# A two-layer kernel: gen's product between qk's halves, av's first half a step later, spread weights a step sooner, turns by transposes, k and v without padding

## The chip, the core and the metric

One core of a Trainium2 chip runs the whole program. Its engines work side by side, each through its own instructions in order: PE (matrix products; PEld is its weight load), DVE (elementwise work and reductions), ACT (scalar functions and copies), POOL (here it issues the gathers) and SP (here it issues DMAs). They wait for each other by semaphores. The metric is device time in microseconds (us) of one execution; the median of the runs is compared. The profile is of one more execution, and its records give each instruction's start and duration.

## What is computed

The input x has 8 images of 256 channels and 64 x 64 positions, in float32. Two layers, each x + f(norm(x)), norm being a group norm over 32 groups:

```python
# layer 0, per image: attention over 3 x 3 windows plus a generated 3 x 3 convolution, 4 heads
qkv = einsum('oc,bchw->bohw', w_qkv, norm(x));  q, k, v = split(qkv)
logits = einsum('bhdl,bhdkl->bhkl', q, patches(k));  attn = softmax(logits, axis=2)
kernel = einsum('hkc,bhcl->bhkl', w_kg, qkv grouped by head) + b_kg
out = alpha * einsum(kernel, patches(v)) + beta * einsum(attn, patches(v))
x = x + einsum('oc,bchw->bohw', w_proj, out)
# layer 1, per image: a deformable 3 x 3 convolution
om = conv3x3(norm(x), w_off) + b_off            # 18 offsets and 9 masks per position
v  = bilinear sample of norm(x) at 9 shifted places (4 corners each), times sigmoid(mask)
x  = x + einsum('bckhw,ock->bohw', v, w)
```

## The kernel before

**Tiling.** An image lies in SBUF as two tiles of 128 channels (`ct`, `m`) by 4096 positions. Both layers go through it in 8 chunks `c` of 8 rows (512 positions, 4 blocks of 128, or 8 squares of 8 x 8 in attention).

**Layer 1** works in *slots*: 72 per image, one for each chunk and each of the 9 places of the window. Per slot, POOL issues four gathers (`gather`, L820: 128 positions with four corners of 256 channels each), ACT scales the first corner (`scale`, L836), DVE adds the other three (`sum_corners`, L844, three instructions for each of two blocks, six in a group), PE turns the four blocks (`transposes`, L865, eight transposes called pt), ACT copies them to vt (L868), and PE multiplies by the weights (`product`, L890, po). At the end of a chunk po is copied to y (L901), added to the residual (L906) and stored.

**Layer 0** (class `Attention`) has per chunk: `q` (L304), `k` and `v` (`keyed`, L336, each in two steps of four rows, 66 columns wide with the padding), `products` (L375) in two halves, sixteen small products each, whose results two DVE products (L383) mask into qk, `logits` (L394 to L403, DVE), `generated` (gen, L409, and its copy gs, L417), softmax in three parts, `turned` (gt, L427, four products with a constant that also adds the two channel tiles up, and DVE's addition of the bias, L435, to kb), `weights` (L495), `spread_weights` (wk, four products L508 and four DVE products L516), `keys` (transposes of v, L531, copied by ACT, L536), `weighted` (av, L549, in two halves) and `project` (L561, added by DVE, L572).

**Order.** The program's order on PE, ACT, DVE and POOL is written out by hand. `attention` and `prepare` (which puts the normed image into the gather table, computes offsets, L702, turns them, L718, and finds `positions`, L735 and on) are generators; each `yield` ends a step, 144 steps an image. The loop at the end puts one step of the *next* image into each half-slot, behind that half's `ahead` (two scales, six sums, two gathers) and `product`. In the loop's first image a step more is taken now and then, until the steps are 12 ahead (`STEPS_AHEAD`). A chunk's attention has 14 steps and so 7 slots; some parts of chunk c-1 (`d`) are done in the steps of chunk c. Before the loop, the first image's 144 steps run alone (the prologue).

The steps of a chunk before are: spread weights of d; q; k(0); k(1); products(0); products(1) with d's first av; logits with d's keys(1); generated, softmax_1; v(0); d's second av, turned; v(1), softmax_3; project(0); weights, project(1); keys(0).

**PSUM.** All of layer 0's products take their banks in turn from a pool of four (`psum_a`): a product waits until the fourth bank before it has been read. pt has two banks, po two.

Of the kernel before, what the change touches and what calls it, by code (L numbers as in the profile page):

```python
# [17 lines left out]
P = 128  # L18
# [5 lines left out]
R = 8  # L24
# [28 lines left out]
STEPS = 2 * SLOTS  # L53
STEPS_AHEAD = 12


@with_exitstack
def preact_kernel(ctx: ExitStack, tc: tile.TileContext, a: dict, out: bass.AP):
# [52 lines left out]
    gmat = const_tile("gmat", [P, P])  # L111
    bkg = const_tile("bkg", [P, HEADS * KK])
    w_qkvT = const_tile("w_qkvT", [P, NT, 3 * C])
# [9 lines left out]
    b_off = const_tile("b_off", [P, 1], nc.sync)  # L123
    stk_om = const_tile("stk_om", [P, NOM], nc.sync)
    stk_gen = const_tile("stk_gen", [P, HEADS * KK], nc.sync)
    base = const_tile("base", [P, NC * NB, 2 * KK], nc.sync)
# [15 lines left out]
    kt = const.tile([P, NT, R + 2, WP], F32, tag="k", name="k")  # L142
    vt = const.tile([P, NT, TC, KT, KT], F32, tag="v", name="v")

    w_effT = const.tile([P, NT, P // 2], F32, tag="w_effT", name="w_effT")
# [116 lines left out]

    def tiled(ps, rows):

        t = ps[:, : rows * WP].rearrange("p (r w) -> p r w", w=WP)
        t = t[:, :, 0 : TC * T].rearrange("p r (t x) -> p t r x", x=T)
        ap = [list(d) for d in t.ap]
        ap[-1][1] = KT
        return bass.AP(tensor=t.tensor, offset=t.offset, ap=ap)

# [19 lines left out]
    class Attention:  # L290
# [37 lines left out]

        def keyed(self, which, i, to):

            for lo, hi in [(0, 2)] * (self.c == 0 and i == 0) + [(2 + 4 * i, 6 + 4 * i)]:
                for m in range(NT):
                    ps = psum_a(f"ps{'qkv'[which]}_{self.u}_{lo}_{m}")
                    o = which * C + m * P
                    for ct in range(NT):
                        nc.tensor.matmul(  # L336
                            ps[:, : (hi - lo) * WP],
                            w_qkvT[:, ct, o : o + P],
                            self.xn[:, ct, lo:hi, :],
                            start=(ct == 0),  # L340
                            stop=(ct == NT - 1),
                        )
                    to(m, lo, hi, ps)

        def k(self, i):
            self.keyed(
                1,
                i,
                lambda m, lo, hi, ps: nc.scalar.copy(
                    kt[:, m, lo:hi, :].rearrange("p r w -> p (r w)"), ps[:, : (hi - lo) * WP]  # L350
                ),
            )

        def v(self, i):
            self.keyed(
                2,
                i,
                lambda m, lo, hi, ps: nc.scalar.copy(vt[:, m, :, lo:hi, :], tiled(ps, hi - lo)),
            )

# [44 lines left out]
        def generated(self):  # L405

            ps = psum_a(f"gen_{self.u}")
            for ct in range(NT):
                nc.tensor.matmul(  # L409
                    ps[64 * ct : 64 * ct + 64, :],  # L410
                    w_effT[:, ct],
                    window(self.xn, ct, 4),
                    start=True,
                    stop=True,
                )
            self.gs = gs = p1.tile([P, N], F32, tag="gs", name=f"gs_{self.u}")
            nc.scalar.copy(  # L417
                gs.rearrange("p (t y x) -> p y t x", y=T, x=T),
                ps.rearrange("p (y t x) -> p y t x", y=T, x=T),
            )  # L420

        def turned(self):

            ps = psum_a(f"gt_{self.u}")
            n = HEADS * KK
            for j in range(NB):
                nc.tensor.matmul(  # L427
                    ps[:, j * n : (j + 1) * n],
                    self.gs[:, j * P : (j + 1) * P],
                    stk_gen,  # L430
                    start=True,
                    stop=True,
                )
            self.kb = kb = p1.tile([P, self.G, KK], F32, tag="kb", name=f"kb_{self.u}")
            nc.vector.tensor_add(  # L435
                kb.rearrange("p (j h) k -> p j (h k)", j=NB),
                ps[:, : NB * n].rearrange("p (j k) -> p j k", j=NB),
                bkg.unsqueeze(1).to_broadcast([P, NB, n]),
            )
# [146 lines left out]
    def attention(b):  # L586
# [12 lines left out]
        for c in range(NC):  # L599
            a_ = Attention(b, c, xn, stats)  # L600
            if d:
                d.spread_weights()
            yield None
            a_.q(0)
# [6 lines left out]
            a_.products(0)  # L611
            yield None
            a_.products(1)
            if d:
                d.weighted(0)
            yield None
            a_.logits()
            if d:
                d.keys(1)
                d.carry_v()  # L620
            yield None
            a_.generated()
            a_.softmax_1()
# [21 lines left out]
            yield None  # L645
            a_.keys(0)
            yield None
            d = a_
        d.spread_weights()
        yield None  # L650
# [19 lines left out]
    def prepare(b, gn):  # L670
# [43 lines left out]
        def positions(c, om):  # L714
            u = f"{b}_{c}"
            ps = psum_a(f"omt_{u}")
            for j in range(NB):
                nc.tensor.matmul(  # L718
                    ps[:, j * NOM : (j + 1) * NOM],
                    om[:, j * P : (j + 1) * P],  # L720
                    stk_om,
                    start=True,
                    stop=True,
                )
            omt = ps[:, : NB * NOM].rearrange("p (b o) -> p b o", o=NOM)
            S = [P, NB, 2 * KK]

            def small(name, shape=S, dt=F32):
                return p1.tile(shape, dt, tag=name, name=f"{name}_{u}")

            mk = small("mk", [P, NB, KK])
            nc.scalar.activation(mk, omt[:, :, 18:27], AF.Sigmoid)
# [138 lines left out]
    def product(b, n, m):  # L871

        c, k = divmod(n, KK)
        if k == KK // 2 and m == 0:
            r = p1.tile([P, NT, N], F32, tag="r", name=f"r_{b}_{c}")
            if b + 1 < B:
                nc.sync.dma_start(r, kept[b % 2][:, :, c * N : (c + 1) * N])
            state["r"] = r
        if k == 0 and m == 0:

            if b + 1 == B and c % 2:
                state["po"] = [psum_a(f"po_{b}_{c}_{i}") for i in range(NT)]
            else:
                po = ps_o.tile([P, NT, 512], F32, tag="o", name=f"po_{b}_{c}")
                state["po"] = [po[:, i, :] for i in range(NT)]
        po, v = state["po"], state["v", n]
        if m == NT - 1:
            del state["v", n]
        for ct in range(NT):
            nc.tensor.matmul(  # L890
                po[m],
                w_conv[:, ct, k, m * P : (m + 1) * P],
                v[:, ct, :],
                start=(k == 0 and ct == 0),
                stop=(k == KK - 1 and ct == NT - 1),
            )

    def finished(b, c, m):
# [4 lines left out]
    def stored(b, c, m=slice(0, NT)):  # L903
        r, y = state["r"][:, m], state["y"][:, m]
        x1 = r if b + 1 < B else image[:, m, c * N : (c + 1) * N]
        nc.vector.tensor_add(r, y, x1)  # L906
        nc.sync.dma_start(
            out[b].rearrange("(t p) l -> p t l", p=P)[:, m, c * N : (c + 1) * N], r
        )
# [7 lines left out]
    with tc.manual_schedule(engines=ordered):  # L917
# [4 lines left out]
        steps = fronts()  # L922
        done = 0
        while done < STEPS:
            next(steps, None)
            done += 1
        for i in range(GATHERS):
            gather(i)
        for i in range(0, SUM_AHEAD, 2):
# [6 lines left out]
            gather(i + GATHERS)  # L936
            gather(i + GATHERS + 1)
        gather(SUM_AHEAD + GATHERS)
        gather(SUM_AHEAD + GATHERS + 1)
        last = None  # L940
        for n in range(B * SLOTS + 1):
# [3 lines left out]
            for m in range(NT):  # L945
# [16 lines left out]
                h = NT * n + m + 1  # L962
                goal = h * STEPS + min(h, STEPS) * STEPS_AHEAD
                while (done - STEPS) * STEPS < goal:
                    next(steps, None)
# [3 lines left out]
def _constants():  # L969
# [16 lines left out]
    turn_x = turns[p % T % 3]  # L986
    stk_om = np.zeros((P, NOM), f)
    for g in range(4):
        stk_om[32 * g : 32 * g + NOM] = np.eye(NOM, dtype=f)
    base = np.zeros((P, NC * NB, KK, 2), f)  # L990
# [8 lines left out]
        "turn_x": turn_x,  # L999
        "stk_om": stk_om,  # L1000
        "stk_gen": np.tile(np.eye(P // 2, HEADS * KK, dtype=f), (2, 1)),
        "base": base.reshape(P, NC * NB, 2 * KK),
# [4 lines left out]
def _laid_out(x, w_qkv, w_kg, b_kg, alpha, beta, w_proj, w_off, b_off, w):  # L1007
# [3 lines left out]
    boff = np.zeros((P, 1), np.float32)  # L1011
    boff[:NOM, 0] = b_off
    return {
        "x": x.reshape(x.shape[0], C, L),
        "w_qkvT": w_qkv.reshape(3 * C, NT, P).transpose(2, 1, 0),
        "w_qkv": w_qkv.reshape(8, 96, C).transpose(1, 0, 2),
        "w_kgT": w_kg.reshape(HEADS, KK, 2, 96).transpose(3, 0, 2, 1).reshape(96, 8, KK),
        "bkg": np.broadcast_to(b_kg.reshape(1, HEADS * KK), (P, HEADS * KK)),
        "alpha": np.broadcast_to(alpha.reshape(1, 1), (P, 1)),
# [26 lines left out]
```

## Time and profile before

| | |
|---|---|
| three timed runs | 5461.75, 5472.33, 5480.27 us; median 5472.33 |
| the profiled execution | 5417.27 us, its span 5415.5 us |
| granted PE clock, mean | 0.942 |
| first product of layer 1 | at 332.6 us |
| image 0 in layer 1 (image 1 in layer 0) | 665.0 us |
| images 1 to 6 in layer 1 | 3900 us, 650 each |
| image 7 in layer 1, nothing beside it | 517.4 us |

Busy time by stage, us (the mean clock and DMA share behind):

| stretch | PE | DVE | ACT | POOL | clock | DMA |
|---|---|---|---|---|---|---|
| 0 to 310 | 273.2 | 178.9 | 101.3 | 2.5 | 0.98 | 0.28 |
| 332.6 to 997.6 | 615.7 | 529.4 | 313.9 | 376.5 | 0.95 | 0.76 |
| 997.6 to 4897.6 | 3576.7 | 3108.8 | 1818.3 | 2218.9 | 0.95 | 0.77 |
| 4897.6 to 5415 | 379.3 | 351.0 | 207.2 | 362.2 | 0.85 | 0.76 |

How to read what follows. A line of groups names the source line, engine, operation, the tiles written and read, shapes and count, then busy time, mean duration of one and idle time before it. Durations of PE overlap, so its cost is better read from one start to the next. A float32 product stands in the trace as two records, a transpose as one. The idle time before an instruction stands in brackets with what ended it; "issue" is time in which the engine waited for nothing that the profile shows, "remote" a signal that the profile cannot put down to an engine.

### The profile page before, as it was taken

What the parts mean: (1) busy time and instruction counts of PE and PEld (TensorE: products, weight loads), DVE (VectorE), ACT (ScalarE), POOL (GpSimd) and SP (SyncE); (2) the same over time, 40 slices, a digit from 0 to 9 for tenths busy, and PEclk for the clock granted to TensorE, in tenths of its full rate; (3) what the DMA queues carried; (4) which work ended last, traced back from release to release, by engine and by line L of the source; (5) the groups of instructions that cost most, each with busy time, mean ns of one, the idle gap of its engine ahead of it and who ended that gap; (6) DMA issues with size and microseconds to landing.
All of it is one profiled execution on the core that took longest, in us unless ns stands there. A gap on an engine that the chain in (4) does not pass through costs nothing. (4 is left out here: it accounts for less than half of the span.)

```text
span 5415.5 us, 80013 instructions
## 1 busy us (share of the span) xinstructions
PE 4849.9 (90%) x26848; PEld 2762.1 (51%) x26848; DVE 4185.3 (77%) x10066; ACT 2447.4 (45%) x5312; POOL 2976.4 (55%) x2310
## 2 busy tenths in 40 slices
PE   8989999999898999999999998989999899987777
PEld 5545554555545555555555555455554555543333
DVE  5577878787787877878788787877878787777666
ACT  3344444444444444444444444444444444444343
POOL 0045554655555556455555555565654655656776
PEclk9999999999999999999999999999999999998888
DMA  2177779777697778877788777877779777688877
GB/s 91 55 253 259 253 244 330 245 249 271 242 330 270 254 264 286 307 249 262 251 310 286 265 256 256 313 266 263 260 244 332 249 248 265 235 288 307 306 268 264
DMA packets 472650, 1414.24 MB, mean 261 GB/s; under 512 B 46815, under 2 KB 114655, under 8 KB 472109
## 3 DMA queue, kind: packets, MB, share of 16 engines
q0 software_dynamic: 331776, 1208.11, 63.4%
q1 hardware_dynamic: 138444, 197.65, 10.3%
q8 instruction: 211, 3.46, 0.2%
q10 hardware_dynamic: 2016, 3.38, 0.2%
q14 instruction: 203, 1.65, 0.1%
HBM read 1276.02 MB, written 132.94 MB: 260 GB/s over the span
## 5 line engine op out<-in xcount | busy, mean ns | idle before, releaser
L820 POOL DMA_INDIRECT g<-table,idx x2304 | 2973.9, 1291 | 2418.0 <-DVE s L844 808.9
L844 DVE SCALAR_TENSOR_TENSOR s<-g,wt,s 128x256 f32<-128x256 f32 x6912 | 2811.7, 476 | 307.6 <-ACT s L836 240.7
L890 PE MATMUL po<-vt,w_conv 128*128 128x512 f32 x4608 | 2255.0, 616 | 33.9 <-ACT y L901 22.4
L836 ACT ACTIVATE s<-g,wt 128x256 f32<-128x256 f32 x2304 | 1068.2, 510 | 574.8 <-DMA g<-table,idx 471.4
L890 PEld LDWEIGHTS po<-vt,w_conv 128*128 128x128 f32 x4608 | 842.0, 198 | 816.8 <-issue 760.1
L868 ACT COPY vt<-pt 128x512 f32<-128x512 f32 x1152 | 618.2, 588 | 528.9 <-PE pt L865 352.5
L865 PE MATMUL pt<-ident,s 128*128 128x128 f32 x4608 | 698.1, 294 | 170.1 <-ACT vt L868 125.6
L865 PEld LDWEIGHTS pt<-ident,s 128*128 128x128 f32 x4608 | 569.3, 151 | 402.6 <-ACT vt L868 166.3
L383 DVE TENSOR_TENSOR qk<-qk,near_k 128x400 f32<-128x400 f32 x256 | 135.4, 567 | 545.8 <-remote 445.7
L375 PE MATMUL qk<-k,q 64*64 64x100 f32 x4096 | 207.4, 268 | 166.5 <-issue 162.1
L304 PE MATMUL psq<-xn,w_qkvT 128*128 128x512 f32 x512 | 258.4, 650 | 65.0 <-DVE wk L516 63.5
L556 ACT COPY acc<-av 128x512 f32<-128x512 f32 x128 | 75.1, 587 | 483.3 <-PE av L549 337.4
L702 PE MATMUL om<-xn,w_off 128*32 128x512 f32 x2304 | 288.6, 596 | 0.6 <-DVE pos L735 0.5
L375 PEld LDWEIGHTS qk<-k,q 64*64 64x64 f32 x4096 | 137.0, 139 | 291.3 <-issue 253.5
L336 PE MATMUL psv<-xn,w_qkvT 128*128 128x264 f32 (+1 forms) x1088 | 259.5, 383 | 0.0
L336 PE MATMUL psk<-xn,w_qkvT 128*128 128x264 f32 (+1 forms) x1088 | 254.5, 379 | 0.0
L336 PEld LDWEIGHTS psv<-xn,w_qkvT 128*128 128x128 f32 x1088 | 201.5, 191 | 85.3 <-issue 49.5
L336 PEld LDWEIGHTS psk<-xn,w_qkvT 128*128 128x128 f32 x1088 | 201.7, 190 | 82.6 <-issue 38.8
L561 PE MATMUL proj<-acc,w_projT 128*128 128x512 f32 x512 | 240.8, 593 | 0.7 <-ACT acc L556 0.7
L549 PEld LDWEIGHTS av<-wk,vk 100*64 100x64 f32 x4096 | 166.0, 163 | 97.9 <-issue 39.9
L549 PE MATMUL av<-wk,vk 100*64 100x64 f32 x4096 | 190.3, 253 | 26.9 <-issue 21.6
L312 ACT COPY q<-psq 128x512 f32<-128x512 f32 x128 | 74.0, 584 | 310.6 <-PE psq L304 310.6
(94 smaller groups left out, 3397.8 us busy)
## 6 DMA issues: line engine op xcount, KB each, us to landing
table<-ts SPq DMA_DIRECT2D x384, 176.0 KB
g<-table,idx POOLq DMA_INDIRECT x2304
out_dram<-r SPq DMA_DIRECT2D x63, 512.0 KB
x<-in_x_dram SPq DMA_DIRECT2D x61, 512.0 KB
x<-x SPq DMA_DIRECT2D x56, 512.0 KB
r<-x SPq DMA_DIRECT2D x56, 512.0 KB
w_conv<-in_w_conv_dram SPq DMA_DIRECT2D x1, 2304.0 KB
x<-in_x_dram ACTq DMA_DIRECT2D x3, 512.0 KB
```

The costliest lines, as they stand in the source:

```text
L304: nc.tensor.matmul(ps, w_qkvT[:, ct, m * P : (m + 1) * P], window(self.xn, ct, 4), start=(ct == 0), stop=(ct == NT - 1),)
L336: nc.tensor.matmul(ps[:, : (hi - lo) * WP], w_qkvT[:, ct, o : o + P], self.xn[:, ct, lo:hi, :], start=(ct == 0), stop=(ct == NT - 1),)
L375: nc.tensor.matmul(both[h][64 * t : 64 * t + 64, n : n + NK], self.qt[r, ct, o * T * T : (o + 1) * T * T], kt[r, ct, :, T * o : T * o + KT ...
L549: nc.tensor.matmul(av[64 * h : 64 * h + 64, g, t * T * T : (t + 1) * T * T], self.vk[:, t, o : o + 64], self.wk[2 * g + h][:, i * n + t * ...
L561: nc.tensor.matmul(ps, w_projT[:, ct, m * P : (m + 1) * P], self.acc[:, ct].rearrange("p (t y x) -> p y t x", y=T, x=T), start=(ct == 0), ...
L702: nc.tensor.matmul(ps[32 * g : 32 * g + 32, :], w_off[:, ct, k, :], window(xn, ct, k), start=(n < 4), stop=(n >= KK * NT - 4),)
L820: nc.gpsimd.indirect_dma_start(out=g, out_offset=None, in_=tables[b % 2], in_offset=bass.IndirectOffsetOnAxis(ap=found[b, c][0][:, j, k : ...
L836: nc.scalar.activation(s, g[:, 0:C], AF.Copy, scale=w[:, 0:1])
L844: nc.vector.scalar_tensor_tensor(s, g[:, q * C : (q + 1) * C], w[:, q : q + 1], s, ALU.mult, ALU.add)
L865: nc.tensor.transpose(pt[ct][:, j, :], s[:, ct * P : (ct + 1) * P], ident)
L868: nc.scalar.copy(v[:, ct, :], pt[ct].rearrange("p b n -> p (b n)"))
L890: nc.tensor.matmul(po[m], w_conv[:, ct, k, m * P : (m + 1) * P], v[:, ct, :], start=(k == 0 and ct == 0), stop=(k == KK - 1 and ct == NT - 1),
```

## The change

- `k` and `v` compute one channel tile per step, all eight rows at once and 64 columns wide (512 columns), instead of both tiles for four rows and 66 columns. The padding of kt and vt is set to zero once by two memsets on POOL. k is copied by one ACT copy, v by two (the six inner squares and the two outer ones).
- `turned` and `positions` turn by four transposes instead of four products with a stacked identity; the groups are added by a DVE reduction. For kb the bias now comes with ACT's copy of gs (so bkg is one column). The constants `stk_om` and `stk_gen` go.
- The steps of a chunk: q; k(0); k(1); products(0); generated; products(1); logits with d's first av; d's keys(1), softmax_1; v(0); and on as before; keys(0) with the chunk's own spread weights.
- Of the 12 steps ahead, 8 (`STEPS_FIRST`) are taken before the loop: four before the first gathers, four between the first sums.
- In the last image the residual is added by PE (a product of the identity and the image's tile, into po), and y is stored without DVE's addition.

```diff
@@ keyed, k, v
-        def keyed(self, which, i, to):
-            for lo, hi in [(0, 2)] * (self.c == 0 and i == 0) + [(2 + 4 * i, 6 + 4 * i)]:
-                for m in range(NT):
+        def keyed(self, which, m, to):
+            for lo, hi in [(0, 2)] * (self.c == 0) + [(2, R + 2)]:
...
-                            ps[:, : (hi - lo) * WP],
-                            self.xn[:, ct, lo:hi, :],
+                        ps[:, : (hi - lo) * W],
+                        self.xn[:, ct, lo:hi, 1 : W + 1],
...
+                nc.scalar.copy(
+                    vt[:, m, 1 : TC - 1, lo:hi, :], strided(ps, T, TC - 2, T - 1, KT)
+                )
+                nc.scalar.copy(
+                    strided(vt[:, m, 0, lo:hi, :], (TC - 1) * NK - 1, 2, 1, KT - 1),
+                    strided(ps, W - KT + 1, 2, 0, KT - 1),
+                )
@@ turned (positions likewise, with four groups of 27)
-                nc.tensor.matmul(
-                    ps[:, j * n : (j + 1) * n], self.gs[:, j * P : (j + 1) * P], stk_gen,
...
+                nc.tensor.transpose(
+                    ps[:, j * P : (j + 1) * P], self.gs[:, j * P : (j + 1) * P], ident
+                )
...
-            nc.vector.tensor_add(
+            nc.vector.tensor_reduce(
                 kb.rearrange("p (j h) k -> p j (h k)", j=NB),
+                ps.rearrange("p (j c k) -> p j k c", j=NB, c=NT)[:, :, 0:n],
+                AX.X,
+                ALU.add,
@@ attention
-            if d:
-                d.spread_weights()
-            yield None
             a_.q(0)
             a_.q(1)
...
             a_.products(0)
             yield None
+            a_.generated()
+            yield None
             a_.products(1)
+            yield None
+            a_.logits()
             if d:
                 d.weighted(0)
             yield None
-            a_.logits()
             if d:
                 d.keys(1)
                 d.carry_v()
-            yield None
-            a_.generated()
             a_.softmax_1()
...
             a_.keys(0)
+            a_.spread_weights()
             yield None
@@ product, stored
+        if b + 1 == B and k == KK - 1:
+            x1 = image[:, m, c * N : (c + 1) * N]
+            nc.tensor.matmul(po[m], ident, x1, start=False, stop=True)
...
-        r, y = state["r"][:, m], state["y"][:, m]
-        x1 = r if b + 1 < B else image[:, m, c * N : (c + 1) * N]
-        nc.vector.tensor_add(r, y, x1)
+        r = state["y"][:, m]
+        if b + 1 < B:
+            r, y = state["r"][:, m], r
+            nc.vector.tensor_add(r, y, r)
@@ before the loop
+        for n in range(STEPS_FIRST - 4):
+            next(steps, None)
         for i in range(GATHERS):
             gather(i)
...
             gather(i + GATHERS + 1)
+            for n in range(2 if i == 0 else 1):
+                next(steps, None)
+        done = STEPS + STEPS_FIRST
```

## The prediction

> **What bounds the kernel now.** I read the page's busy shares first, then the table of waits, then PE's, DVE's and POOL's timeline of one attention chunk, then the busy time by stage.
>
> ```profile
> PE 4849.9 (90%) x26848; PEld 2762.1 (51%) x26848; DVE 4185.3 (77%) x10066; ACT 2447.4 (45%) x5312; POOL 2976.4 (55%) x2310
> ```
> ```profile
> DVE qk L383 <- remote: 445.7, 65, 11.3
> ...
> PE qk L375 <- issue: 162.1, 245, 1.8
> ...
> PE psq L304 <- DVE wk L516: 63.5, 41, 3.1
> ```
> PE looks like the bound, yet two of these waits belong together and do not look like a full PE: DVE waits for the first half of qk, 445.7 us in 65 waits, and PE itself is idle inside qk with nothing shown as its reason. One chunk, PE:
>
> ```profile
> 2393.85 0.94 PE L375 MATMUL qk<-k,q 64*64 64x100 f32 x32
> 2394.71 1.98 PE L890 MATMUL po<-vt,w_conv 128*128 128x512 f32 x4
> 2396.63 0.58 PE L375 MATMUL qk<-k,q 64*64 64x100 f32 x16
> 2398.15 0.36 PE L375 MATMUL qk<-k,q 64*64 64x100 f32 x3 [0.94 <-issue]
> ...
> 2403.01 1.97 PE L549 MATMUL av<-wk,vk 100*64 100x64 f32 x32
> ```
> The first half runs in 0.94 us; the second starts at 2396.63 and ends only at about 2403; av right behind it takes 1.97 us, where the other av of a chunk takes 1.15, because the clock fell to half. DVE and POOL meanwhile:
>
> ```profile
> 2381.40 9.75 DVE L844 SCALAR_TENSOR_TENSOR s<-g,wt,s 128x256 f32<-128x256 f32 x24
> 2401.02 0.57 DVE L383 TENSOR_TENSOR qk<-qk,near_k 128x400 f32<-128x400 f32 x1 [9.87 <-remote]
> ```
> ```profile
> 2381.45 7.97 POOL L820 DMA_INDIRECT g<-table,idx  x1 [0.30 <-issue]
> 2389.72 1.06 POOL L820 DMA_INDIRECT g<-table,idx  x1 [0.30 <-DVE s L844]
> ```
> DVE runs 24 corner sums without a break; under them one gather takes 7.97 us instead of 0.94. Then POOL catches up with a train of 9 gathers, 1.245 us apart, until 2400.7. PE finished the first half of qk at 2394.8, but DVE sees its signal only at 2401.0, 6.2 us late. In the prologue, with no gathers, the same signal takes 0.05 us. So the signal (and, behind it, the next burst of small matmuls) is held up while the gather train runs. Over the chunks, the lag is 6.1 to 8.7 us where the half starts 3.5 to 5.5 us into the train, and 1.9 to 4.9 where it starts less than 3.5 us into it (one chunk at 406 us apart).
>
> ```profile
> 2381.50:2401.00 19.50, 16.99 (x109) 9.90 (x108) 9.57 (x24) 8.37 (x18) 16.47 (x10) 1.00 0.78 263
> 2401.00:2444.90 43.90, 42.11 (x221) 24.83 (x222) 38.92 (x90) 20.12 (x45) 19.32 (x19) 0.92 0.72 248
> ```
> Columns: length, then busy PE, PEld, DVE, ACT, POOL. Cut at the same marks (end of DVE's wk products, start of its first qk product), the chunks behind the first prologue average 19.3 us for the first stretch (A; DVE busy 9.9) and 42.6 for the second (B; DVE 38.8, PE 40.2). B is DVE and PE together, nearly full. A is where a chunk loses time: DVE idles some 9.4 us for one late signal. A chunk is A + B = 61.9 us, and there are 56 (7 batches of 8).
>
> **The change, part by part.** Base: the profiled execution, 5417.27 us (span 5415.5 and 1.8 around it). The three timed runs have a median of 5472.33, 55 us more; I carry these 55 unchanged.
>
> *PE work.*
> ```profile
> L336 PE MATMUL psv<-xn,w_qkvT 128*128 128x264 f32 x1024 | 252.2, 390 | 0.0
> ...
> L561 PE MATMUL proj<-acc,w_projT 128*128 128x512 f32 x512 | 240.8, 593 | 0.7 <-ACT acc L556 0.7
> ...
> L531 PE MATMUL vk<-ident,v 128*100 128x128 f32 x1024 | 134.4, 275 | 0.0
> ...
> L427 PE MATMUL gt<-stk_gen,gs 128*128 128x36 f32 x512 | 69.3, 282 | 2.2 <-ACT v L358 2.1
> ```
> A product is two records; a transpose is one. k and v: 16 records of 264 columns each a chunk become 8 of 512. From start to next start, 264 columns take 223 to 233 ns and 512 take 433 (proj): 16 x 0.228 - 8 x 0.433 = 0.18 us each, 0.36 a chunk; by columns alone (528 against 512) 0.22. I take 0.3. Turned: 8 records at 113 ns become 4 transposes at 110 (L531): 0.45 a chunk. Positions: the same 0.45 per chunk of prepare. Together 64 x 1.2 = 77 us of PE, of which only what lies on A, B or a PE-bound stage counts.
>
> *DVE work.* The add of kb (0.31 us) becomes a reduction of 288 elements, between L452 (144 elements, 0.29) and L466 (432, 0.60): 0.45, so +0.15 a chunk. Positions gain a reduction of 432 elements: +0.6 (L466), bounds 0.5 to 0.7 (L400). ACT: k goes from four copies at 0.38 to two at about 0.59 (L349, L868), v stays at four; gs gains a bias, 0.69 instead of 0.59. ACT is 45% busy; nothing taken. The one queue effect: mk on ACT now waits for DVE's reduction; copies of vt queue behind it. Bounded with the prepare stage below.
>
> *Prologue.* Eight chunks start 25.4 us apart with PE nearly full: 8 x 0.75 = -6; prepare there 8 x 0.45 = -3.6. At its end PE stands idle 10.4 + 2.3 us before the first transposes; eight of the twelve steps ahead (norm, q, k, first half of qk: some 9 us of PE) now run there instead of inside batch 0: -9, bounds 0 and -12.6. Sum -19. The two memsets on POOL (about 1.2 us each, by L140) lie under the input's load; two small loads fall away.
>
> *A (56 times).* The spread weights move ahead of q by a step. q's wait for their banks (63.5 us in all, 1.1 a chunk) goes; in its place the third and fourth spread product stand behind ACT's copies of vk, two of 0.59 us (L536), which were covered by a half-slot before: about 1 us, on PE behind a DVE that is late there anyway. Through the shift by one step, one run of eight transposes (0.87 us) fewer lies between q and the first half. From the end of the wk products to the first half I get 11.0 us instead of 12.4, so 2.7 us into the train instead of 4.1. There the rows with 1.5 to 3.2 us show lags of 2.9 to 4.9; I take 3.9. New A: 11.0 + 0.9 + 3.9 = 15.8, so -3.5. Bounds: lag 0.05 (prologue), so -7.3; or the train's end decides as now, 0.
>
> *B.* The halves now stand 6.2 us apart (transposes 0.87, gen 1.0, two po 1.72 each, 0.93) instead of 2.8; av stands 3.5 behind the second half. With q and k on four banks, the second bank of the second half is that of the first half: PE must now wait for DVE's first qk product. DVE reaches it 4.8 us after the half has started, so no wait; if the lag stays 7, PE waits some 2 us. DVE has two groups of sums (2.45 each) to do before it needs the second half; its signal, again late by 3 to 6, costs about 0.5. kb +0.15. B: +0.6, bounds -1 (kb's own wait, 3.8 in most chunks, shrinks with fewer records before it) and +3.
>
> A + B: -2.9 x 56 = -162.
>
> *Prepare, batches 1 to 7.* PE -3.6, DVE +4.8 a batch; between 2200 and 2250 us PE is busy 47.6 of 50, DVE 46.0, the DMA engines 91%. I take 0; bounds -25 and +34 in all.
>
> *Last batch.* 7.2 us per slot, PE 73%, DVE 69%: 16 identity products (two records of about 0.49) are +16 us of PE, the residual adds (L906, 1.21 x 8) -10 of DVE. Both lie beside gathers: 0, bounds -10 and +16.
>
> Sum: 5417 - 19 - 162 = 5236; with the 55, 5291; I say 5290 us.
>
> **A rule against the change.** The Trainium skill, TensorE: Matmul & The Clock Gate, Part 4: PE-mode transpose, says that transposes do not count as busy for the clock gate. As a mechanism here: turned's window would fall to half clock. A half-clock stretch in this trace is 3.41 us, so 64 x 3.41 / 2 = 109 us would come back: 5400. Against it: at 2370.88 eight transposes of vk and eight of s run back to back, 1.75 us, at full clock.
>
> **Rivals.** (1) The signal stays tied to the end of the gather train. For: in chunks at 8 us into the train the release still comes 2 us after the last gather. Then A and B stay, and the prologue's 19 and perhaps a third of the PE work remain, -45: 5427. (2) The hold-up dissolves, as bursts no longer follow each other. A is 12.0; PE's own 57 us a chunk then bounds, less what half clock added: -6.4 x 56 - 19: 5095. Against: gathers and their train are untouched, and a half alone (2645 us) has stalled too. (3) Slower: the new bank tie. If the first half's signal is still 7 us late, PE stops at the second half for DVE, and av, 3.5 us behind it, meets the hold-up a second time (in the first batch halves 3.6 apart stalled by 5 to 7 us). It decides once the lag passes 5.3 us; price A unchanged, B +3: +168 - 19, 5621. (4) The clock rule: 5400.
>
> **Chances.** Forecast 0.42 (own range 5210 to 5380), (1) 0.25, (2) 0.18, (3) 0.10, (4) 0.05. A measurement of this kernel tells some 0.3% (16 us) from no change. Of (1), 0.05 falls within it and 0.02 above. So faster 0.83, same 0.05, slower 0.12. The range, 5110 to 5455, leaves out (3) and the lower part of (2).
>
> **What would show it.** Right: DVE's wait at the first qk product falls from 6.9 to about 4 us each; PE's idle time inside qk falls by at least half; q's wait for wk vanishes; A near 16, B near 43; records of turned halve at 110 ns. Wrong: the wait at the first qk product keeps its 446 us (rival 1), PE shows a wait for DVE at the second half or for issue at av (rival 3), or half clock follows the transposes of gt.

## The result, and the profile after

| | before | changed |
|---|---|---|
| median | 5467.04 us (5460.02 to 5480.27, 4 runs) | 5261.59 us (5256.95 to 5263.70, 4 runs) |
| ratio | | 0.9618, 95% interval 0.9598 to 0.9639 |
| profiled execution | 5417.27 us | 5263.70 us |
| first product of layer 1 | 332.6 us | 336.2 us |
| images 0 to 6 in layer 1 | 4565.0 us | 4389.4 us |
| image 7, to the end of the span | 517.9 us | 536.3 us |
| A, mean of the 49 short ones | 19.27 us | 17.35 us |
| B, mean of 56 | 42.63 us | 41.56 us |

A runs from the end of a chunk's wk products to DVE's first product on the next qk, B from there to the end of the next wk products; the short ones leave out the seven that cross from one image to the next.

The kernel is 3.8% faster. Between the two profiled executions 153.6 us are gone: +3.6 ahead of layer 1, -175.6 in images 0 to 6, +18.4 in the last image. A and B together lose 2.99 us a chunk, 167 us in 56 chunks.

The busy time of the changed kernel, from the first part of its page:

```profile
PE 4784.5 (91%) x25344; PEld 2471.7 (47%) x25344; DVE 4216.5 (80%) x10121; ACT 2412.2 (46%) x5200; POOL 2882.2 (55%) x2312
```
PE does 65 us less, and DVE 31 us more, in a shorter span: the shares alone would not tell that an idle stretch went. The changed kernel's table of waits does (engine and line, what it waited for, us in all, times, longest):

```profile
DVE qk L388 <- remote: 130.0, 25, 8.6
...
DVE qk L388 <- PE gen L414: 118.5, 25, 7.0
...
DVE qk L388 <- PE qk L380: 68.7, 17, 10.8
...
DVE qk L388 <- PE pt L870: 52.9, 17, 8.5
...
PE wk L512 <- DVE x L576: 34.4, 34, 1.5
...
PE qk L380 <- issue: 18.8, 22, 3.3
...
PE psq L306 <- DVE wk L520: 5.4, 10, 2.6
```
The wait that stood under one name (445.7 us, remote) is now spread over four names, because other PE work stands behind the first half when its late signal comes. By instruction rather than by name, DVE's wait at its first product on the first half adds up to 442.8 us before and 313.1 after, 7.9 and 5.6 a chunk. PE's idle time inside qk falls from 162.1 to 18.8, q's wait for wk from 63.5 to 5.4. A new small one is that of the spread products, L512, for the bank that the addition of proj (L576) still reads.

One chunk of the changed kernel, DVE:

```profile
2366.64 2.47 DVE L520 TENSOR_TENSOR wk<-wk,near 100x512 f32<-100x512 f32 x4
2369.04 7.19 DVE L849 SCALAR_TENSOR_TENSOR s<-g,wt,s 128x256 f32<-128x256 f32 x18
2379.28 2.46 DVE L849 SCALAR_TENSOR_TENSOR s<-g,wt,s 128x256 f32<-128x256 f32 x6 [3.04 <-ACT s L841]
2387.31 1.05 DVE L388 TENSOR_TENSOR qk<-qk,near_k 128x400 f32<-128x400 f32 x2 [5.57 <-PE gen L414]
...
2394.17 1.04 DVE L388 TENSOR_TENSOR qk<-qk,near_k 128x400 f32<-128x400 f32 x2
```
PE in the same chunk:

```profile
2381.58 0.94 PE L380 MATMUL qk<-k,q 64*64 64x100 f32 x32
...
2385.18 1.08 PE L414 MATMUL gen<-xn,w_effT 128*64 128x512 f32 x4
...
2388.11 0.93 PE L380 MATMUL qk<-k,q 64*64 64x100 f32 x32
...
2392.88 1.15 PE L553 MATMUL av<-wk,vk 100*64 100x64 f32 x32
```
And POOL:

```profile
2371.83 5.22 POOL L825 DMA_INDIRECT g<-table,idx  x1 [2.58 <-DVE s L849]
2377.35 0.94 POOL L825 DMA_INDIRECT g<-table,idx  x1 [0.30 <-ACT vt L873]
...
2385.00 0.94 POOL L825 DMA_INDIRECT g<-table,idx  x1 [0.30 <-issue]
```
The first half ends on PE at 2382.5 and reaches DVE at 2387.31: still 4.8 us late, 1.4 us behind the end of a train of 7 gathers (2377.35 to 2385.9). But the second half now runs in 0.93 us where it took 6, av in 1.15 instead of 1.97, and DVE finds the second half ready. Over the chunks the lag's median falls from 6.1 to 4.3 us. The second half takes 1.67 us in the mean instead of 5.04. Cut at A's and B's marks:

```profile
2369.00:2387.30 18.30, 18.30 (x87) 8.81 (x86) 9.70 (x25) 7.00 (x14) 12.22 (x9) 1.00 0.67 225
2387.30:2428.70 41.40, 39.17 (x227) 20.28 (x226) 40.11 (x91) 22.19 (x49) 21.86 (x20) 1.00 0.86 292
```
The clock (the third column from the end) is 1.00 in this B, where it was 0.92 in the one shown of the kernel before. Time at half clock falls from 629.8 to 541.0 us in all.

The groups that the lighter products touch (busy time, mean ns of one, idle before):

```profile
L337 PE MATMUL psv<-xn,w_qkvT 128*128 128x512 f32 (+1 forms) x576 | 248.2, 557 | 2.1 <-DVE kb L438 2.1
...
L512 PE MATMUL wk<-wsb,spread 9*100 9x512 f32 x512 | 143.6, 676 | 34.6 <-DVE x L576 34.4
...
L434 PE MATMUL gt<-ident,gs 128*128 128x128 f32 x256 | 43.9, 297 | 0.0
```
v goes from 259.5 to 248.2 us, k from 254.5 to 246.3, turned from 69.3 to 43.9; the spread products rise from 77.7 to 143.6.

### The profile page after: what moved, and what is told of

Same layout as the page of the kernel before. It is cut to its first block, busy times and chain, and to the rows that moved or that the text cites. A ratio compares the mean times of both kernels' runs of the same rounds, so it can differ in the third digit from the quotient of the medians.

```text
span 5261.9 us, 76801 instructions
## 1 busy us (share of the span) xinstructions
PE 4784.5 (91%) x25344; PEld 2471.7 (47%) x25344; DVE 4216.5 (80%) x10121; ACT 2412.2 (46%) x5200; POOL 2882.2 (55%) x2312
## 3 DMA queue, kind: packets, MB, share of 16 engines
q0 software_dynamic: 331776, 1208.11, 65.2%
## 5 line engine op out<-in xcount | busy, mean ns | idle before, releaser
L825 POOL DMA_INDIRECT g<-table,idx x2304 | 2877.1, 1249 | 2358.6 <-DVE s L849 845.4
L337 PE MATMUL psv<-xn,w_qkvT 128*128 128x512 f32 (+1 forms) x576 | 248.2, 557 | 2.1 <-DVE kb L438 2.1
L337 PE MATMUL psk<-xn,w_qkvT 128*128 128x512 f32 (+1 forms) x576 | 246.3, 557 | 0.0
L540 ACT COPY vk<-vk 100x512 f32<-100x512 f32 x256 | 137.1, 587 | 120.2 <-PE vk L535 113.7
L256 DVE TENSOR_SCALAR xn<-x,gn 128x576 f32<-128x576 f32 (+2 forms) x256 | 176.6, 731 | 0.0
L553 PEld LDWEIGHTS av<-wk,vk 100*64 100x64 f32 x4096 | 131.6, 139 | 94.6 <-issue 40.8
L512 PE MATMUL wk<-wsb,spread 9*100 9x512 f32 x512 | 143.6, 676 | 34.6 <-DVE x L576 34.4
L306 PEld LDWEIGHTS psq<-xn,w_qkvT 128*128 128x128 f32 x512 | 99.7, 199 | 155.9 <-issue 103.0
L704 PEld LDWEIGHTS om<-xn,w_off 128*32 128x32 f32 x2304 | 74.2, 109 | 200.6 <-issue 164.1
L348 ACT COPY k<-psk 128x512 f32<-128x512 f32 (+1 forms) x144 | 79.2, 550 | 192.7 <-PE psk L337 185.9
```

Of the source, the lines that this page charges most:

```text
L256: nc.vector.tensor_scalar(xn[:, ct, o : o + hi - lo, 1 : W + 1], xt[:, ct, lo * W : hi * W].rearrange("p (r w) -> p r w", w=W), gn[:, 0, c ...
L306: nc.tensor.matmul(ps, w_qkvT[:, ct, m * P : (m + 1) * P], window(self.xn, ct, 4), start=(ct == 0), stop=(ct == NT - 1),)
L337: nc.tensor.matmul(ps[:, : (hi - lo) * W], w_qkvT[:, ct, o : o + P], self.xn[:, ct, lo:hi, 1 : W + 1], start=(ct == 0), stop=(ct == NT - 1),)
L512: nc.tensor.matmul(ps[:NK], spread[32 * h : 32 * h + KK], self.wsb[32 * h : 32 * h + KK], start=True, stop=True,)
L704: nc.tensor.matmul(ps[32 * g : 32 * g + 32, :], w_off[:, ct, k, :], window(xn, ct, k), start=(n < 4), stop=(n >= KK * NT - 4),)
L825: nc.gpsimd.indirect_dma_start(out=g, out_offset=None, in_=tables[b % 2], in_offset=bass.IndirectOffsetOnAxis(ap=found[b, c][0][:, j, k : ...
```

## The experiments

A fact that no run had shown before stands over all of them: they ran on four chips, and these showed two kinds of behaviour. The kernel before takes 5426 us on one of them, near the result's 5467, and 4832 to 4849 on the other three. On the chips of the second kind the first half's signal comes at most 0.1 us after the half in 45 of 56 chunks (e1) and 49 of 56 (e11), and at most 1.0 us in any; "holds signals up" below means the first kind. Each chip of the experiments was used in one stretch of time only, so the runs cannot tell a lasting property of the chip from a state that it was in; "kind of chip" means what was seen then. So each time is set beside the runs of the kernel before on its own chip. With the changed kernel on a chip of the second kind (e11), DVE's waits for qk have no entry by remote any more, and the largest is an ordinary one for PE's work:

```profile
DVE qk L388 <- PE qk L380: 183.7, 102, 10.5
```

| run | chip | us | before there | ratio, 95% |
|---|---|---|---|---|
| e1 order undone | 1 | 4774.7 | 4832.3 | 0.9887 (0.9870 to 0.9903) |
| e2 gen undone | 1 | 4795.1 | 4832.3 | 0.9926 (0.9908 to 0.9944) |
| e3 av undone | 1 | 4791.7 | 4832.3 | 0.9915 (0.9898 to 0.9932) |
| e4 spread undone | 1 | 4909.2 | 4832.3 | 1.0159 (1.0142 to 1.0176) |
| e5 changed | 2, holds up | 5201.3 | 5426.3 | 0.9580 (0.9542 to 0.9618) |
| e6 before, profile | 2, holds up | 5413.8 | 5426.3 | one run |
| e7 order alone | 2, holds up | 5234.7 | 5426.3 | 0.9645 (0.9599 to 0.9691) |
| e8 residual undone | 2, holds up | 5198.6 | 5426.3 | 0.9589 (0.9549 to 0.9628) |
| e9 before, small gathers | 3 | 4786.1 | 4840.4 | one run |
| e10 late mask | 3 | 4833.8 | 4840.4 | 0.9990 (0.9978 to 1.0002) |
| e11 changed | 3 | 4797.6 | 4840.4 | 0.9921 (0.9897 to 0.9945) |
| e12 changed, small gathers | 4 | 4805.1 | 4849.4 | one run |

**e1 to e4: parts of the order undone.** Each starts from the changed kernel.

```diff
# e1: all three
+            if d:
+                d.spread_weights()
+            yield None
             a_.q(0)
...
             a_.products(0)
             yield None
-            a_.generated()
-            yield None
             a_.products(1)
+            if d:
+                d.weighted(0)
+            yield None
+            a_.logits()
...
+            a_.generated()
             a_.softmax_1()
...
             a_.keys(0)
-            a_.spread_weights()
# e2: generated() back with softmax_1
# e3: weighted(0) back into the step of products(1)
# e4: spread_weights() at the head of the next chunk's q, in its step
```


> The changed kernel with the old order of a chunk's steps (gen with the first part of the softmax, av's first half with the second half of qk, spread weights at the start of the next chunk); the lighter products, transposes, prologue and last image stay as changed. Theory (the order brings the gain, by an earlier and shorter hold-up of the first half's signal): A goes back to 19.3 us, B stays within 1 us of the changed kernel's 41.6, q waits for the wk products again, and the time is 5262 + 56 x 2 to 3 = 5375 to 5430 us. Rival (the smaller PE work brings it, 77 us and what hangs on it): the time stays within 30 us of 5262.

> The changed kernel with gen alone put back behind the logits, so that the two halves of qk are adjacent steps again; av and the spread weights stay where the change put them. Theory (two bursts of small products inside one hold-up stall PE): PE's idle time inside qk goes back from 29 us to over 100, A stays near 17.4 because the first half stands where it stood, B grows by 1 to 2 us: 5320 to 5375 us. Rival (the distance of the halves is beside the point, since DVE is the bound in B): 5250 to 5280 us.

> The changed kernel with av's first half alone put back into the step of the second half of qk. Theory: the second half no longer meets the hold-up, so av right behind it does not either; DVE waits for the logits' inputs no longer than before: within 20 us of 5262. Rival (the later av is what unblocks PE after the halves): PE idle at av goes up from 0.4 us to over 20, and 5300 to 5340 us.

> The changed kernel with the spread weights alone put back by a step, to the start of the next chunk's q. Theory (what counts is how long after the wk products the first half comes, against the gather train): the four products and q's wait for their banks come between the end of the run of transposes and q again, the wk products end later against the first half, but DVE's own work before the run of sums moves with them; A goes back to 18 to 19.3 us and the time to 5300 to 5370 us. Rival (the wait of q is covered, the gain comes from gen between the halves alone): within 20 us of 5262.

The expected times were for the wrong kind of chip, and none of the four times came true; what can be read is the ratios and the stretches. With all of the order undone the kernel is still 1.1% faster than the one before: A is 13.65 us (49 short ones), B 40.14, and the median lag 0.05. Beside the changed kernel on another chip of this kind (e11, 0.9921) the old order is no worse. So the order brings nothing that these runs show where the signal is on time; the two kernels ran on two chips and are compared by their ratios. e2 and e3, with one part undone each, are at 0.9926 and 0.9915, within their intervals of e11. PE's idle time in qk and at av, which e2 and e3 were to bring back, does not come back: PE waits 1.9 us in all inside qk in e2, and 0.5 us at av in e3. On such a chip the distance of the halves is thus worth nothing by itself; on the other kind the single parts were not tried.

e4 is the one that hurts, 2.4% above e11 by the ratios. In its table of waits:

```profile
PEld psq L306 <- DVE wk L520: 164.7, 97, 4.3
...
PE psq L306 <- DVE wk L520: 102.9, 48, 3.4
```
In e11 the first of these is 25.6 us and the second 0.6. A does not go back to 18 or 19 us, as expected, but stays at 13.58; B rises to 42.85. With gen's step between the halves, the spread weights have no step of their own any more; in front of q in one step, q's products wait for DVE to empty four banks. The spread weights' place is not a gain in itself: it is what makes room for gen's step (e1, with an own step for them, does not pay it).

**e5 to e7: the changed kernel, the kernel before and the order alone, on a chip that holds signals up.** e7 has the kernel before with the attention's steps of the changed one and nothing else of it. The chip was one that holds signals up, so what e5 and e6 expected of the other kind was not tested by them.

> The changed kernel itself once more, beside the kernel before on the same chip, since e1 to e4 ran on a chip on which the kernel before takes 4832 us instead of 5467 and the first half's signal comes 0.0 to 0.1 us after the half in every chunk (A 13.2 to 14.0 us). Theory (the order pays only through the signal that is held up): on such a chip the order gives nothing, A and B are those of e1 (13.2 and 40.3 us) within 1 us, and the time is 4770 to 4800 us, with the kernel before at 4832. Rival (the order pays by itself, through gen between the halves): under 4740 us. If the chip is one that holds the signal up: 5262 beside 5467.

> The kernel before once more, for its profile on this chip. Theory: no DVE wait by remote at the first half, lag under 0.2 us, gathers in trains of 4 or 5 instead of 9 to 12, A about 13.5 us, granted clock 0.98. Rival (the faster chip has the same late signal and gains elsewhere): lag of 4 to 8 us and A near 19.

> The kernel before with the new order of a chunk's steps alone (gen between the halves, av's first half with the logits, spread weights with keys(0)); k, v, turned, positions, prologue and last image as before. Theory: on a chip that holds the signal up 5467 - 56 x 2 to 3 = 5300 to 5355 us; on one that does not, within 30 us of 4832. Rival (the order needs the lighter products to pay): slower than the kernel before by over 30 us on either chip.

The order alone takes 191.5 us off, 3.6% (interval 3.1 to 4.0); the whole change 225.0. The rest, 33 us, is a difference of two medians whose runs spread over 30 us each. A and B are 19.60 and 42.17 in e6, 17.52 and 40.84 in e7, 16.72 and 41.68 in e5: -3.4 us a chunk in both, 191 and 189 in 56. The profiled executions differ by 185 and 196 us. The median lag goes 6.1 to 4.6 and 3.5. The kernel before, DVE's waits:

```profile
DVE qk L383 <- remote: 460.3, 64, 11.4
```
and with the order alone:

```profile
DVE qk L383 <- remote: 170.4, 28, 8.5
DVE qk L383 <- PE gen L409: 138.3, 23, 8.1
DVE qk L383 <- PE qk L375: 69.7, 18, 11.3
```
By instruction, DVE's wait at the first half falls from 454.9 to 335.3 us. So on such a chip the order carries most of the gain, as it did in the forecast; it took off more than the 112 to 168 us expected. Which of its three moves does it there was not tried on a chip of this kind and stays open.

**e8: the last image's residual by DVE again.**

```diff
-        if b + 1 == B and k == KK - 1:
-            x1 = image[:, m, c * N : (c + 1) * N]
-            nc.tensor.matmul(po[m], ident, x1, start=False, stop=True)
...
+        r, y = state["r"][:, m], state["y"][:, m]
+        x1 = r if b + 1 < B else image[:, m, c * N : (c + 1) * N]
+        nc.vector.tensor_add(r, y, x1)
```


> The changed kernel with the last image's residual added by DVE again (no identity products, r written by DVE before the store). Theory (the 16 identity products, 17.8 us of PE, and the wait of po for ACT's y are what made the last image 18 us longer): 10 to 18 us less than the changed kernel on the same chip, all of it behind the last image's first product. Rival (the last image is bound by its gathers, and is longer because the first prologue's steps no longer lie ahead of it or by chance): within 5 us of the changed kernel.

The 10 to 18 us less that were expected did not come: the medians, 5198.6 and 5201.3, do not differ. In the profiled executions the last image takes 509.8 us instead of e5's 532.6, and e6 and e7, which have no identity products either, take 523.0 and 522.7. So three traces without these products lie 10 to 23 us below the one with them, which suggests that they make the last image longer on this kind of chip; the time does not show it.

**e9 and e12: gathers of a quarter of the bytes.** e9 from the kernel before, e12 from the changed one.

```diff
-            out=g,
+            out=g[:, 0:C],
...
-                    s, g[:, q * C : (q + 1) * C], w[:, q : q + 1], s, ALU.mult, ALU.add
+                    s, g[:, 0:C], w[:, q : q + 1], s, ALU.mult, ALU.add
```


> The kernel before with each gather cut to a quarter of its bytes (one corner of 256 channels per position instead of four; the corner sums read that one corner again, so layer 1's output leaves the other three corners out); as many gathers, packets and DVE instructions as before. Theory (the first half's signal is held up by the data that the train of gathers moves, not by the number of gathers): the lag after the first half falls from a median of 6.1 us to under 1 us, A from 19.5 to about 13, and the last image, bound by its gathers, falls from 518 to about 380 us. Rival (the issue of the gathers, POOL's instructions and their descriptors, holds the signal up): lag stays at 4 us or more in trains of 9.

> The changed kernel with each gather cut to a quarter of its bytes, as in e9 (layer 1's output leaves out three of four corners). Theory on a chip that holds signals up (before 5400 or more): with the DMA engines seldom full the signals are no longer late, the lag after the first half falls from a median of 3.4 us to under 0.5, A from 16.7 to 13 to 14 us, the last image from 528 to about 385 us, and the whole from 5200 to 4780 to 4830 us, the time of a chip without the hold-up. Rival there (it is the issue of gathers, not their bytes): lag over 2 us, A over 16, over 5100 us. On a chip that does not hold them up (before about 4835): A and B as in e11 (13.6 and 40.6 us), and the last image near 384 us as in e11 instead of the 413 of e9, if the identity products and not the gathers make that difference; near 413 if not.

Both leave out three of four corners, so their output is not the kernel's. Both fell on chips that do not hold signals up, so whether the bytes make the hold-up was not decided. (The gathers' packets fell too, from 331776 to 110592, against what was written.) What they do show: a quarter of the traffic leaves A at 13.43 and 13.62 and B at 40.08 and 40.43, where e1 and e11 with all of it have 13.65 and 13.60, 40.14 and 40.46. So on these chips the gathers' data costs layer 0's chunks next to nothing. The last image takes 418.1 us in e9, where 380 were expected, and 421.0 in e12, longer than e11's 389.2 with all bytes; the expectation that the identity products bring e12 to 384 failed.

**e10 and e11: DVE's products on the first half a step later, and the changed kernel beside it.**

```diff
             a_.products(0)
             yield None
+            a_.masked(0)
             a_.generated()
             yield None
             a_.products(1)
+            a_.masked(1)
```
(`masked` holds the two DVE products that stood at the end of `products`; the residual is as in e8.)

> The changed kernel with DVE's two products on the first half of qk put a step later, behind the next six corner sums, and the last image's residual added by DVE as before the change. Theory (on a chip that holds the signal up, DVE stands idle some 3.4 us for it in the median while 2.5 us of corner sums are ready behind it): DVE's wait at the first half falls by about 2.4 us a chunk, 56 x 2 = 110 us, and the last image by 20 us: 5070 to 5110 beside 5201 for the changed kernel and 5426 for the one before. Rival (with 30 sums in one run the gathers are issued later still, the train grows and the second half meets it): within 20 us of the changed kernel or slower. On a chip without the lag: no gain but the last image's, within 25 us of the changed kernel.

> The changed kernel once more as the measure for the other two on this chip. Theory: on a chip that holds the signal up 5200 to 5262 us beside 5426 to 5467; on one that does not (before 4832), 4770 to 4800 us, A 13.2 to 13.9 us and B 40.3 us, so that only the 20 to 60 us of lighter work are left of the gain. Rival: under 4740 us there.

e11 measures what the change is worth without the hold-up: 0.8% (interval 0.55 to 1.03), 42.8 us, instead of 3.8%. e10 is 36 us slower than e11, more than the 25 us expected. Its DVE wait at the first half goes from 96.3 us to 0, and the one at the second half from 30.0 to 68.3. Images 1 to 5 together last 2917.5 us in e10 and 2914.6 in e11, and the 28 us more in the last image (417.5 against 389.2) are nearly all of the difference between the profiled executions. So filling DVE's idle time at the first half gains nothing on such a chip; whether it pays on the other was not tried. No variant ran on both kinds.

**What the two kinds of chip do differently, from their traces.** DVE's, PE's and ACT's signals and the DMAs' landings are semaphore updates, each with its time. The same program must make the same updates, but the trace of the changed kernel holds 50029 of them and e11's 65332 (33321 and 45595 from DMAs). All six traces of chips that hold signals up have 49660 to 50210, all eight of the others 65253 to 65435. So about a quarter of the updates stands in no record of its own on the first kind. In the microseconds in which 100 gather packets or more start (the DMA engines are then about full) the changed kernel's trace has 8.7 updates per microsecond and e11's 16.1; with so many unrecorded, this is not the rate at which signals pass. The count tells the two kinds apart, but not when the missing signals came. The start of an instruction that was waiting needs no such record, and the late starts are what the argument rests on. On both kinds some 390 KB per microsecond pass in these full stretches. In the changed kernel's last image, with no attention at all beside it, POOL issues gather upon gather:

```profile
5029.82 0.94 POOL L825 DMA_INDIRECT g<-table,idx  x1 [0.30 <-issue]
...
5036.20 0.94 POOL L825 DMA_INDIRECT g<-table,idx  x1 [0.30 <-issue]
5044.49 1.26 POOL L825 DMA_INDIRECT g<-table,idx  x1 [7.35 <-ACT s L841]
```
while ACT gets nothing:

```profile
5029.93 0.51 ACT L841 ACTIVATE s<-g,wt 128x256 f32<-128x256 f32 x1 [0.78 <-issue]
5040.17 1.07 ACT L873 COPY vt<-pt 128x512 f32<-128x512 f32 x2 [9.73 <-remote]
```
PE had ended these transposes at 5027.3. From 5024 to 5039 some 400 KB pass per microsecond, and one or two updates are recorded; ACT starts at 5040.17, as the gathers' packets run out, some 13 us after its input was done. The same image as a whole, the changed kernel on the result's chip and e11 (length, busy PE, PEld, DVE, ACT, POOL, clock, DMA share, GB/s):

```profile
4725.60:5262.00 536.40, 386.22 (x1170) 194.18 (x1168) 341.11 (x836) 204.96 (x436) 359.27 (x271) 0.85 0.73 276
```
```profile
4401.90:4791.00 389.10, 358.17 (x1170) 168.62 (x1168) 343.63 (x837) 210.93 (x436) 274.15 (x272) 1.00 0.97 383
```
The same program moves 383 GB/s with the engines 97% busy on one chip, and 276 at 73% on the other: there the DMA engines idle between trains. The lines above show such a pause: POOL waits 7.35 us for ACT, and ACT 9.73 us for the late signal. That the gathers' traffic is what delays the updates is read from these traces, and not shown by an experiment; why only some chips do it stays open. Since the records are missing on the very chips that hold signals up, it is open too whether the making of the trace has a part in it. A slower clock alone is not the difference between the kinds: the changed kernel's PE is at half clock for 541.0 us on the result's chip and 128.8 in e11, which by an estimate costs PE at most half of these 412 us, 206, and the medians lie 464 us apart.

## Why the prediction was right, and where its steps were off

**The bound.** Right for chips that hold signals up: the late signal was the place, and the order of steps the lever (e7). Wrong in its generality: the profile of one chip could not tell that others have no hold-up. On three of the experiments' four chips only 0.8% are left (e11), and the old order does as well there (e1).

**A, forecast 15.8 us, came to 17.35 (-1.9 instead of -3.5).** The step that failed is "from the end of the wk products to the first half I get 11.0 us instead of 12.4": the median of the short ones is 12.4 in both. q's wait and a run of transposes did go from this stretch, but the half came no earlier. What moved is the train of gathers. Counted anew after every pause of 0.4 us and every gather of 2.5 us or more, it starts 8.2 us behind the wk products in the median where it was 7.0, has 7 gathers where it had 9, and so ends 16.8 us behind them instead of 19.2. A goes the same way, 17.35 and 19.27. On the other chip that holds signals up the train's end goes from 19.2 (e6) to 16.8 (e7 and e5), and A from 19.60 to 17.52 and 16.72. In e1, where signals are on time, the train ends 24.7 us behind the wk products and A is 13.65. So, as the traces read, A shrank because the train ended earlier and not because the half came earlier; no run moved the train's end alone to show it. That the lag was 4.3 us, near the 3.9 taken, is luck. The recorded working could have seen it: its rows of lag by place in the train cover the 29 chunks whose half starts within 5.5 us of the train's start, and leave out 27 that start later, with lags of 0.7 to 8.2 us. In 47 of the 56 chunks of the kernel before, the release comes 0 to 2.3 us behind the train's last gather. Why two gathers fewer pile up in the new order was not taken apart.

**B, forecast +0.6, came to -1.1.** The step "its signal, again late by 3 to 6, costs about 0.5" failed: DVE's wait at the second half falls from 0.68 to 0.12 us a chunk, with two groups of sums between its products on the two halves, whose starts are 5.7 us apart. (On the chip of e6 and e5 it is 0.33 and 0.37, so there it did not fall.) And the unstalled second half and av at full clock, not counted, took PE's time down (40.2 to 39.1 busy). The sum of A and B, -2.99, met the -2.9 only because the two errors cancel; that is luck.

**PE work.** By the groups k and v gave 0.30 and turned 0.40 us a chunk (19.5 and 25.4 us over 64 chunks), about the 0.3 and 0.45 that were taken. In the prologue the chunks come 25.05 us apart instead of 25.45, so -0.40 where -0.75 was written. The products of wk cost more in their new place: from one start to the next, waits included, 73.8 us become 176.9, 1.6 a chunk, where the working had about 1.

**Prologue, forecast -19.** The first product of layer 1 comes 3.6 us later, not earlier, and images 0 to 6 gain only 8 us beyond A and B. On the other chip, e5 and e8, with the eight steps ahead, reach image 1 at 970.6 and 977.2 us, e7 without them at 977.8. The -9 for steps run in the gap is not to be seen.

**Spread weights.** The wait was put on ACT's copies of vk at about 1 us a chunk; most of it is on DVE's addition of proj, 34.4 us in all, 0.6. With the spread weights left at q's step the kernel is over 2% slower on a chip without the hold-up (e4).

**Last image, forecast 0, bounds -10 to +16: +18.4.** e8's profile points to the identity products (22.8 us less without them; e6 and e7, also without, 10 less), e10 beside e11 to the opposite on another kind of chip (28 us more without them; e1 to e4 and e11, all with them, take 388 to 392). It is the place with the largest error and the least settled.

**The 55 us** between the profiled execution and its runs were carried to the changed kernel, whose profile and runs agree within 2 us. Without them the sum was 5236 for 5264, with them 5290 for 5262: too much gain by 27 us, in the prologue and the last image, hidden by an offset that did not carry over.

**The rivals.** (1), the signal tied to the train's end: its time was wrong, as A fell, but its mechanism is the one that the traces bear out; it took the train to stay as it was, and the train got shorter. (2), the hold-up dissolves: it did so on three chips, but by the chip and not by the change; A and B together are then 54.1 us (e11), below the 57 that were taken for PE alone. (3), the bank tie: PE waits for DVE at the second half for 7.4 us in all; no. (4), the clock rule of the Trainium skill, TensorE: Matmul & The Clock Gate, Part 4: PE-mode transpose: with 512 transposes in the place of products (256 in turned, 256 in positions) time at half clock fell by 89 us, and in the 4.5 us from the start of gt's transposes no half-clock stretch begins in any of the 64 chunks (one in the kernel before). This trace does not agree with it as a mechanism here.

## What to carry to other kernels

A wait whose releaser the profile cannot name, on an instruction whose producer has long ended, can be a late signal: look at what the DMA engines do then. Here the signal came as a train of gathers ended, so what made the train end earlier paid, and a second burst moved away from the first ran without its stall. Before a change is judged by a few per cent, run the kernel before on more than one chip: here the same two kernels differ by 3.8% on one and 0.8% on another. And moving a step frees it only if the next products do not then stand behind the banks that it fills (e4).

## What the runs showed of the hardware

In these runs chips of the same type differ by 13% in the time of the same kernel (4832 to 5467 us). The granted clock goes with it (0.942 against 0.983), which does not say which leads. Where signals are held up, DVE sees the first half's end 6.1 us late in the median (before), near the end of a train of gathers; elsewhere 0.05 us (e1, e11). With the gathers' data passing at some 390 KB per microsecond on both, only the first kind shows the lag, and its traces lack about a quarter of the semaphore updates. One gather's instruction on POOL takes 0.94 us, but 5.22 us under 18 corner sums of DVE (changed) and 7.97 under 24 (before). Cutting the gathers' bytes to a quarter, on chips without the hold-up, changed a chunk by less than 0.1 us (e12 beside e11).
